# Half of a KAN's activations moved from ScalarE to GpSimd, value tiles cleared once, and a third PSUM bank for the attention's row maxima

## The chip, the core and the metric

The kernel runs on one core of a Trainium2 chip. Its time is device microseconds (us) of that core. The engines are named as in the profile: PE is TensorE's matmul, PEld its weight load, ACT ScalarE, DVE VectorE, POOL GpSimd, SP SyncE (which here only issues DMAs). Each engine works through its own instructions in the order in which the kernel issued them, so an instruction that waits holds up all that stand behind it on its engine.

## What is computed

Sixteen sequences (rows, b = 0 to 15) of 512 tokens with 128 features go through two "macaron" layers. The reference's main lines are:

```
x = x + 0.5 * kan(layernorm(x))                 # s = x@Win + bin; h = relu(s*W1 + b1), 16 values per
                                                # feature; g = sum(h*W2) + b2; out = g@Wout + bout
x = x + attention(layernorm(x))                 # 16 heads of 8, 4 key/value heads, rope, causal softmax
x = x + 0.5 * kan(layernorm(x))
x = x + 0.5 * moe(layernorm(x))                 # 8 experts, each takes its top 128 of 512 tokens
x = x + recurrence(layernorm(x))                # s = l*s + u over the tokens
x = x + 0.5 * moe(layernorm(x))
```

The part that the change touches most is the KAN's inner function, for each of 64 features m with 16 hidden values each:

```
h = relu(s[..., None] * W1 + b1)
g = einsum('btmh,mh->btm', h, W2) + b2
```

Since relu(z + c) = max(z, -c) + c, the sum over h can also be made from max(z, -c), if the sum of c*W2 is added to b2 once.

## The kernel before

**One program of coroutines.** All engine work is issued by Python generators, each of which stands for one stage of one row and gives up its place with `yield`. One round over all of them is a *turn*; `turn()` first issues what was put off to the next turn (`later`, which is where a result leaves PSUM), then steps the urgent stages, then the side stages, then refills a budget per engine. In a turn of the attention phase the main loop (from L1216) steps `weights(b)` and `maxima(b + 1)` once each, and so a row has 4 x 11 = 44 turns. When `paced[0]` is set, a stage that asks with `need(...)` or `bank(...)` for more than the budget has left waits for another turn. The budget of a turn is `MOST = {"pe": 1.5, "dve": 1.15, "act": 0.85, "pool": 1.45}` (L234); the work of `weights` and `maxima` itself isn't in it. After the attention `paced` is off and `hurry` is on.

**Rows in flight.** While `weights(b)` runs, `maxima` works on row b + 1. From turn 38 of row b `stage_in(b + 4)` runs the first KAN and `attn_in` of a later row, and from turn 8 `stage_out(b - 1)` the output projection, the second KAN and the router's scores of the row before. After the 44 turns `finish` makes more turns if `stage_in(b + 2)` isn't through.

**maxima** (L631 to L658): for each of 4 groups of heads, 11 banks of scores are made by bf16 matmuls (L645; L641 first adds the causal mask) and reduced to row maxima by DVE (L650 for a bank of one head, a custom add-and-max with the mask; L655 for shared banks). The banks come from the pool `scp`, which has two; PE can fill a third one only when DVE has read the first. **weights** (L692 to L718) makes the scores a second time, transposed (L709), in two banks of the pool `stp`; ACT takes the exponentials (L712) and POOL sets the masked part of the diagonal block to zero (L714). **outputs** (L720 to L760) multiplies them with the values (L735) a group later.

**kan(b)** (L347 to L409): after a layernorm (L303 to L324; its power of -1/2 runs on POOL, L309 and L310, and the scaling on DVE, L320 or L324), a transpose (L336) and a copy (L338), two matmuls (L356) make both halves of s, each copied to SBUF by ACT (L359). Eight steps follow, spread over 15 turns; each makes one activation of 128x512 on ACT (L389). After the fourth and the eighth step four matmuls (L383) sum four of these values into the bank `ps_kg`, of the pool `kap`, which has one bank and nothing else in it until the experts use it. In the second step POOL adds the constant `kcst` to x (L393). ACT copies the bank to `gT` (L396), four matmuls (L404) project it, DVE adds to x (L405). `kan_held` lets only one KAN at a time have its second half of s.

**attn_in(b)** (L440 to L517): a norm, two matmuls for the query and its rotated form (L448, L454), both multiplied with the rope by DVE (L449, L455) and added by POOL (L470); keys and values (L462, L466). `parts` splits the query and the key into three bf16 terms: a copy on ACT (L414) and three subtractions on POOL (L417, L420, L423). The values go to a fresh tile `va` of four buffers, which POOL first sets to zero (L476), with a column of ones (L479); DVE copies the values in (L484) in the next turn.

**prepare** (L542 on) makes the constants, among them `kcst`, from b2, Wout and bout. **dispatch** (L940 on) transposes gathered tokens for the experts into a PSUM bank `ps_x`: in `ps_kg`'s bank once all KANs are through, in a bank of the shared pool `mm` before that. The pool `mm` has two banks, counted by `held`; nearly all other stages use it.

Of the kernel before, what the change touches and what calls it, by code (L numbers as in the profile page):

```python
# [17 lines left out]
P = 128  # L18
# [30 lines left out]
def tile_macaron(  # L49
# [55 lines left out]
    with ExitStack() as ph:  # L105
# [4 lines left out]
        vap = ph.enter_context(tc.tile_pool(name="p1_va", bufs=4))  # L110
        hp = ph.enter_context(tc.tile_pool(name="p1_h", bufs=5))
# [55 lines left out]
        rbias = cst.tile([P, 2, NV], F32, name="rbias")  # L167

# [36 lines left out]
        ROWS = slice(0, P)  # L205

# [50 lines left out]
        held, kan_held, kans, hurry = [0], [0], [2 * B], [False]  # L257
# [89 lines left out]
        def kan(b):  # L347
# [18 lines left out]
            pg = kap.tile([P, S], F32, name="ps_kg")  # L366
# [3 lines left out]
            for t in range(U + 1):  # L370
                while now[0] < begin + 15 * t // 8:
                    yield
                four = t in (U // 2, U)
                work = {"act": 0.8} if t < U else {}
                if four:
                    work["pe"] = 1.0
                if t == 1:
                    work["pool"] = 1.25
                yield from need(**work)
                if four:  # L380
                    for half, v, h in hs:
                        o = half * M + v % 2 * MH
                        nc.tensor.matmul(pg[o : o + MH, :], lhsT=w2d[:, half, v, :], rhs=h,  # L383
                                         start=(t < U), stop=(t == U))
                    hs = []
                if t < U:
                    half, v = t // 2 % 2, t // 4 * 2 + t % 2
                    h = hp.tile([P, S], F32, name="kan_h")
                    nc.scalar.activation(h, sk[half], AF.Relu, bias=rbias[:, half, v : v + 1],  # L389
                                         scale=kw1[:, half, v : v + 1])  # L390
                    hs.append((half, v, h))
                if t == 1:
                    nc.gpsimd.tensor_tensor(x[b], x[b], kcst.unsqueeze(1).to_broadcast([P, NT, D]), ALU.add)  # L393
                if t == U:
                    gT = hp.tile([P, S], F32, name="kan_h")
                    later.append(lambda: nc.scalar.copy(gT, pg))  # L396
                yield
            take(act=0.6)
            kan_held[0] = 0
            kans[0] -= 1  # L400
# [39 lines left out]
        def attn_in(b, st):  # L440
# [3 lines left out]
            tb = w1p.tile([P, S], F32, name="rope_b")  # L444
# [27 lines left out]
            qp_steps = parts(ta, qpart, nc.scalar.copy, 1.15, act=0.6)  # L472
            step(qp_steps)

            va = vap.tile([P, NT, NR, 32], F32, name="va")
            nc.gpsimd.memset(va, 0.0)  # L476
            mine = [va[:, :, j::2, 2 * HD * j : 2 * HD * (j + 1)] for j in range(2)]
            for to in mine:
                nc.gpsimd.memset(to[:, :, :, HD : HD + 1], 1.0)  # L479
# [10 lines left out]
            st["va"] = va  # L490

            def keys():
# [3 lines left out]
                yield  # L496
                yield
# [44 lines left out]
        def prepare():  # L542

            for half in range(2):
                nc.vector.scalar_tensor_tensor(rbias[:, half, :], in0=kw1[:, half, :], scalar=binc[:, half : half + 1],
                                               in1=kb1[:, half, :], op0=ALU.mult, op1=ALU.add)
            nc.vector.tensor_add(w2d[:, 0, 0:2, :].rearrange("p v m -> p (v m)"), ident[:, 0:M], ident[:, M:P])
# [8 lines left out]
            yield  # L556
            psc = yield from bank([1, D], F32, "ps_kc")
            nc.tensor.matmul(psc, lhsT=kb2, rhs=wout, start=True, stop=True)
# [71 lines left out]

        def maxima(b, st):  # L631
            qp, kp = packed(b)
            for half in range(2):
                maxs = topped[half][:, 0 : NT * NH // 2].rearrange("p (h c) -> p h c", c=NT)
                for r in (2 * half, 2 * half + 1):
                    for c, gs in BANKS:
                        n = (c + 1) * P
                        v = in_bank(scp.tile([P, S], F32, name="ps_sc"), gs)
# [165 lines left out]
        def routing(k, g):  # L804
# [50 lines left out]
            tokf = rtp.tile([P, CAP], F32, name="tokf")  # L855
# [7 lines left out]
            both = rtp.tile([P, 2, P], F32, name="both")  # L863
# [76 lines left out]
        def dispatch():  # L940
            while taken[0] < NR * B:
                yield
            for i in range(0, len(order), 2):
# [5 lines left out]
                own = kans[0] == 0  # L949
                if own:  # L950
# [8 lines left out]
                if not own:  # L959
                    freed()  # L960
# [353 lines left out]
```

## Time and profile before

| | |
|---|---|
| median of 13 runs | 1647.13 us (1639.85 to 1656.4) |
| the profiled execution | 1649.8 us, of which 1646.3 us span |
| busy, share of the span | PE 92%, PEld 64%, DVE 67%, ACT 58%, POOL 57% |
| first exponential (L712), last one | 115.2 us, 937.1 us |
| one row of attention, 349.59 to 403.40 us | 53.81 us: PE 50.11, DVE 42.38, ACT 40.35, POOL 30.30 |
| L389, the KAN's activation, ACT, 128x512 | x256, 816 ns |
| L393, add of kcst, POOL, two inputs, 128x512 | x32, 1277 ns |
| L476, memset of va, POOL, 128x512 | x16, 525 ns |
| L714, mask on POOL, 128x512 and 128x128 | x64, 644 ns and x512, 319 ns |
| L650, maxima on DVE, 128x512 and 128x384 | x256, 682 ns and x256, 549 ns |
| chain that ended last, by engine | PE 70%, DVE 16%, ACT 6%, issue 3%, POOL 3% |

The span is the time from the first to the last instruction of the profiled execution. A group's line in the profile names the line of the kernel, the engine, the operation, output and input, and a count. Busy shares of POOL are rough, and a matmul's end is modelled, so a PE that seems busy may still have gaps. The chain is followed back from the last instruction, at each step to what released it.

### The profile page before, as it was taken

Reading aid. Unit: us, or ns where it says so; the run is one execution under the profiler, and the core shown is the slowest. Engines: PE = TensorE matmul, PEld = TensorE weight load, DVE = VectorE, ACT = ScalarE, POOL = GpSimd, SP = SyncE. Lnnn points to the kernel's source line nnn. Section 1 sums busy time; section 2 is a strip of 40 time slices with the busy share of each in tenths; the row PEclk is TensorE's granted clock in tenths of the full one; section 3 lists DMA queues with packets and bytes.
Section 4 is the critical chain, followed back from the end, with each engine's and each line's share of the span. In section 5 each row is a group of like instructions: output and inputs, shape, how many; then the busy total and the mean of one; then the engine's idle time right before and its main releaser. Section 6 shows DMA issues by size and latency. Waiting matters only on the chain.

```text
span 1646.3 us, 33179 instructions
## 1 busy us (share of the span) xinstructions
PE 1506.7 (92%) x11903; PEld 1052.7 (64%) x11905; DVE 1095.0 (67%) x3574; ACT 957.7 (58%) x1852; POOL 933.1 (57%) x1475
## 2 busy tenths in 40 slices
PE   5678999999999999999989899999999999999998
PEld 2334444445444444444444499899998999889898
DVE  5587878777877788888887255765578555743333
ACT  3345667777777777777767754444453445443343
POOL 2435546555654565456534856556765666666662
PEclk8889999999999999999999999999999999999999
DMA  5311111012101210122022113223222233232332
GB/s 130 88 45 38 45 51 50 20 48 58 49 23 45 58 56 18 44 58 57 26 74 74 30 45 68 64 55 73 63 67 63 61 71 71 62 64 65 65 68 49
DMA packets 107467, 92.87 MB, mean 56 GB/s; under 512 B 23470, under 2 KB 95863, under 8 KB 107063
## 3 DMA queue, kind: packets, MB, share of 16 engines
q1 hardware_dynamic: 84464, 67.67, 14.4%
q0 software_dynamic: 21584, 22.89, 7.6%
q8 instruction: 93, 1.52, 0.4%
q14 instruction: 72, 0.58, 0.1%
q10 hardware_dynamic: 1254, 0.20, 0.1%
HBM read 59.20 MB, written 35.45 MB: 57 GB/s over the span
## 4 chain that ended last, share of the span: by engine, by line
PE 70%; DVE 16%; ACT 6%; issue 3%; POOL 3%; DMA 1%; SPq 1%; another core or an unknown queue 0%; ACTq 0%; DVEq 0%; POOLq 0%
PE ps_y L1041 13%; PE ps_h L1028 13%; PE ps_av L735 7%; DVE below L650 6%; PE ps_st L709 6%; PE ps_sc L645 5%; PE acc L992 5%; PE ps_s L356 3%; PE ps_kg L383 3%; ACT pt L712 3%; PE ps_t L336 3%; DVE ln_st L303 2%; PE ps_x L955 2%; PE ps_g L796 2%; ACT kan_h L389 2%
## 5 line engine op out<-in xcount | busy, mean ns | idle before, releaser
L714 POOL TENSOR_SCALAR_AFFINE_SELECT pt<-pt 128x128 f32<-128x128 f32 (+2 forms) x704 | 256.0, 370 | 346.3 <-ACT pt L712 342.1
L712 ACT ACTIVATE pt<-ps_st 128x512 f32<-128x512 f32 x682 | 366.9, 563 | 116.7 <-PE ps_st L709 115.2
L650 DVE CUSTOM_DVE_ANT_0 below<-ps_sc,causal 128x512 bf16<-128x512 f32 (+1 forms) x512 | 315.3, 616 | 94.8 <-PE ps_sc L645 79.6
L931 POOL DMA_INDIRECT xg<-xnd,tokI x256 | 253.7, 991 | 84.5 <-issue 43.7
L1030 ACT ACTIVATE mo<-ps_h 128x512 f32<-128x512 f32 x256 | 152.8, 597 | 223.0 <-PE ps_h L1028 150.7
L1028 PE MATMUL ps_h<-xin,mw 128*128 128x128 f32 x2048 | 275.9, 277 | 4.9 <-ACT mo L1030 3.0
L1041 PE MATMUL ps_y<-mw,mo 128*128 128x128 f32 x2048 | 273.9, 277 | 6.5 <-DVE ye L1047 5.0
L645 PE MATMUL ps_sc<-kp,qp 96*128 96x512 bf16 (+3 forms) x1024 | 256.2, 302 | 22.2 <-DVE topped L650 17.3
L709 PE MATMUL ps_st<-qp,kp 128*128 128x512 bf16 (+1 forms) x990 | 247.6, 301 | 26.8 <-ACT pt L712 25.1
L1028 PEld LDWEIGHTS ps_h<-xin,mw 128*128 128x128 f32 x2048 | 252.1, 193 | 20.1 <-issue 14.5
L1041 PEld LDWEIGHTS ps_y<-mw,mo 128*128 128x128 f32 x2048 | 251.3, 193 | 10.0 <-DVE ye L1047 6.2
L709 PEld LDWEIGHTS <-kp 128*128 128x128 bf16 x1024 | 94.5, 99 | 186.5 <-issue 167.3
L389 ACT ACTIVATE kan_h<-kan_s,rbias,kw 128x512 f32<-128x512 f32 x256 | 206.9, 816 | 2.2 <-PE ps_kg L383 2.2
L1058 POOL DMA_INDIRECT sum<-mo,tokI x93 | 151.7, 1631 | 90.3 <-issue 26.5
L735 PE MATMUL ps_av<-pt,va 128*32 128x512 f32 (+3 forms) x2048 | 165.7, 441 | 0.8 <-POOL pt L714 0.7
L645 PEld LDWEIGHTS <-qp 96*128 96x128 bf16 x1024 | 95.1, 98 | 102.9 <-issue 79.1
L655 DVE TENSOR_REDUCE topped<-ps_sc 128x2 f32<-128x512 f32 (+1 forms) x192 | 129.7, 687 | 22.0 <-PE ps_sc L645 21.5
L735 PEld LDWEIGHTS ps_av<-pt,va 128*32 128x32 f32 x2048 | 53.4, 109 | 90.5 <-issue 43.3
L310 POOL TENSOR_TENSOR ln_rstd<-ln_rstd,mhalf 128x4 f32<-128x4 f32 x96 | 102.0, 1062 | 8.0
L309 POOL TENSOR_SCALAR ln_rstd<-ln_mv 128x4 f32<-128x4 f32 x96 | 22.1, 230 | 136.8 <-DVE ln_mv L307 134.9
L1047 DVE SCALAR_TENSOR_TENSOR parts<-ps_y,gainT,parts 128x128 fp32r<-128x128 f32 x80 | 27.9, 348 | 98.9 <-ACT parts L1044 76.7
L1047 DVE SCALAR_TENSOR_TENSOR ye<-ps_y,gainT,ye 128x128 fp32r<-128x128 f32 x83 | 29.0, 349 | 89.2 <-ACT ye L1044 61.2
(205 smaller groups left out, 2321.9 us busy)
## 6 DMA issues: line engine op xcount, KB each, us to landing
qp<-qs SPq DMA_DIRECT2D x64, 288.0 KB
xnd<-kan_x SPq DMA_DIRECT2D x32, 256.0 KB
sum<-x SPq DMA_DIRECT2D x62, 128.0 KB
qs<-qpart SPq DMA_DIRECT2D x48, 128.0 KB
kp<-ks SPq DMA_DIRECT2D x48, 96.0 KB
x<-in_L_attn_x_dram SPq DMA_DIRECT2D x16, 256.0 KB
mw<-in_L_ffn_w_dram SPq DMA_DIRECT2D x16, 256.0 KB
xg<-xnd,tokI POOLq DMA_INDIRECT x256
```

The costliest lines, as they stand in the source:

```text
L389: nc.scalar.activation(h, sk[half], AF.Relu, bias=rbias[:, half, v : v + 1], scale=kw1[:, half, v : v + 1])
L645: nc.tensor.matmul(v[:, u, 0:n], lhsT=qp[r][0:MXR, g, bass.ts(c, P)], rhs=kp[0:MXR, r, 0:n], start=alone, stop=(u == len(gs) - 1), skip_gr ...
L650: nc.vector.tensor_tensor_reduce(below[:, 0:n], v[:, 0, 0:n], causal[:, S - n : S], 1.0, LOWEST, ALU.add, ALU.max, accum_out=maxs[:, h, c ...
L709: nc.tensor.matmul(v[:, u, 0:n], lhsT=kp[ROWS, r, bass.ts(c, P)], rhs=qp[r][ROWS, g, c * P : S], start=True, stop=True)
L712: nc.scalar.activation(o, v[:, :, 0:n], AF.Exp, scale=HD ** -0.5)
L714: nc.gpsimd.affine_select(out=dg, in_=dg, compare_op=ALU.is_ge, fill=0.0, base=0, pattern=[[0, len(gs)], [1, P]], channel_multiplier=-1)
L735: nc.tensor.matmul(po[32 * g : 32 * g + 32, c * P : S], lhsT=va[:, c, r, :], rhs=pt[:, g, OFF[c] : OFF[c] + n], start=(c == 0 and not odd) ...
L931: nc.gpsimd.indirect_dma_start(out=xgs[i // E % 2][:, i % E, :], out_offset=None, in_=xnd[b], in_offset=bass.IndirectOffsetOnAxis(ap=tokI[ ...
L1028: nc.tensor.matmul(pst[:, f, :], lhsT=mw1[e][:, bass.ts(f, P)], rhs=xins[i // E % 2][:, i % E, :], start=True, stop=True)
L1030: nc.scalar.activation(hs[u], pst, AF.Gelu)
L1041: nc.tensor.matmul(py, lhsT=hs[u][:, f, :], rhs=mw2[e][:, f, :], start=(f == 0), stop=(f == NF - 1))
L1058: nc.gpsimd.indirect_dma_start(out=sums[k, b], out_offset=bass.IndirectOffsetOnAxis(ap=tokI[g][:, n : n + 1], axis=0), in_=added[b % 2 * ( ...
```

## The change

- **KAN.** Of the eight activations of a KAN the four with odd v are made by POOL as max(W1*s, -c) (by DVE in the last KAN, under `hurry`); the other four stay on ACT. The eight matmuls that sum them all come after the eighth step, four in one turn and four in the next, into a bank of the shared pool `mm` in place of `kap`'s. `hp` holds eight tiles instead of five; `gT` gets a buffer of `kan_s0`. The add of kcst moves from the second to the fifth step.
- **Constants.** `nbias` is -rbias. `prepare` sums c*W2 of the shifted values by four matmuls of one column, doubles that sum (w2d carries a factor of 0.5) and adds b2, and uses the result in b2's place.
- **maxima.** Every third bank comes from `kap`, so three are in rotation. `dispatch` then always uses `kap`'s bank.
- **attn_in.** Four tiles `VA` are fixed; each is set to zero, with its ones, only for rows 0 to 3. The first step of the query's `parts` isn't taken in the turn of POOL's add, but, when paced, two turns later. The key's add then comes one turn later than before and its `parts` two.
- **Buffers.** `rope_b` shares a buffer with `yT`, `tokf` with `probs`, `both` with `wk`.

```diff
-        vap = ph.enter_context(tc.tile_pool(name="p1_va", bufs=4))
-        hp = ph.enter_context(tc.tile_pool(name="p1_h", bufs=5))
+        vap = ph.enter_context(tc.tile_pool(name="p1_va", bufs=1))
+        hp = ph.enter_context(tc.tile_pool(name="p1_h", bufs=8))
...
+        VA = [vap.tile([P, NT, NR, 32], F32, name=f"va{i}", tag=f"va{i}") for i in range(4)]
...
-            pg = kap.tile([P, S], F32, name="ps_kg")
             hs = []
             begin = now[0]
             U = 2 * NV
-            for t in range(U + 1):
+            for t in range(U):
                 while now[0] < begin + 15 * t // 8:
                     yield
...
+                half, v = t // 2 % 2, t // 4 * 2 + t % 2
+                shifted = v % 2
+                yield from need(**({"pool": 0.8} if shifted else {"act": 0.8}))
+                h = hp.tile([P, S], F32, name="kan_h")
+                if shifted:
+                    (nc.vector if hurry[0] else nc.gpsimd).tensor_scalar(
+                        h, sk[half], kw1[:, half, v : v + 1], nbias[:, half, v : v + 1], ALU.mult, ALU.max)
+                else:
                     nc.scalar.activation(h, sk[half], AF.Relu, bias=rbias[:, half, v : v + 1],
                                          scale=kw1[:, half, v : v + 1])
...
-                if t == 1:
+                hs.append((half, v, h))
+                if t == 4:
+                    yield from need(pool=1.25)
                     nc.gpsimd.tensor_tensor(x[b], x[b], kcst.unsqueeze(1).to_broadcast([P, NT, D]), ALU.add)
...
+            pg = yield from bank([P, S], F32, "ps_kg", 1.0)
+            for begins in (True, False):
+                for half, v, h in hs[0:4] if begins else hs[4:8]:
+                    o = half * M + v % 2 * MH
+                    nc.tensor.matmul(pg[o : o + MH, :], lhsT=w2d[:, half, v, :], rhs=h,
+                                     start=begins, stop=not begins)
+                if begins:
+                    yield
+                    yield from need(pe=1.0)
+            gT = w2p.tile([P, S], F32, name="kan_g", tag="kan_s0")
+            later.append(lambda: nc.scalar.copy(gT, pg))
+            kan_held[0] = 0
...
-            qp_steps = parts(ta, qpart, nc.scalar.copy, 1.15, act=0.6)
-            step(qp_steps)
-
-            va = vap.tile([P, NT, NR, 32], F32, name="va")
-            nc.gpsimd.memset(va, 0.0)
+
+            va = VA[b % len(VA)]
             mine = [va[:, :, j::2, 2 * HD * j : 2 * HD * (j + 1)] for j in range(2)]
-            for to in mine:
-                nc.gpsimd.memset(to[:, :, :, HD : HD + 1], 1.0)
+            if b < len(VA):
+                nc.gpsimd.memset(va, 0.0)
+                for to in mine:
+                    nc.gpsimd.memset(to[:, :, :, HD : HD + 1], 1.0)
...
             st["va"] = va
+            if paced[0]:
+                yield
+            qp_steps = parts(ta, qpart, nc.scalar.copy, 1.15, act=0.6)
...
+            psc = yield from bank([P, 1], F32, "ps_kcg")
+            for half in range(2):
+                for v in range(1, NV, 2):
+                    o = half * M + MH
+                    nc.tensor.matmul(psc[o : o + MH, :], lhsT=w2d[:, half, v, :], rhs=rbias[:, half, v : v + 1],
+                                     start=(v == 1), stop=(v == NV - 1))
+            nc.vector.tensor_copy(gcst, kb2)
+            for half in range(2):
+                rows = slice(half * M + MH, (half + 1) * M)
+                nc.vector.scalar_tensor_tensor(gcst[rows, :], in0=psc[rows, :], scalar=2.0, in1=kb2[rows, :],
+                                               op0=ALU.mult, op1=ALU.add)
+            freed()
             psc = yield from bank([1, D], F32, "ps_kc")
-            nc.tensor.matmul(psc, lhsT=kb2, rhs=wout, start=True, stop=True)
+            nc.tensor.matmul(psc, lhsT=gcst, rhs=wout, start=True, stop=True)
...
-                        v = in_bank(scp.tile([P, S], F32, name="ps_sc"), gs)
+                        v = in_bank((kap if turns[0] % 3 == 2 else scp).tile([P, S], F32, name="ps_sc"), gs)
+                        turns[0] += 1
...
-                own = kans[0] == 0
-                if own:
-                    ps = kap.tile([D, 2, CAP], F32, name="ps_x", tag="ps_kg")
-                else:
-                    ps = yield from bank([D, 2, CAP], F32, "ps_x")
+                ps = kap.tile([D, 2, CAP], F32, name="ps_x", tag="ps_sc")
```

## The prediction, made before the changed kernel had run

> **What bounds the kernel now.** I read the page's busy shares and slices first, then the windows of one row of attention, then who waited for whom in four equal rows, the timeline of one row, and the chain of waits beside it.
>
> ```profile
> PE 1506.7 (92%) x11903; PEld 1052.7 (64%) x11905; DVE 1095.0 (67%) x3574; ACT 957.7 (58%) x1852; POOL 933.1 (57%) x1475
> ...
> PE   5678999999999999999989899999999999999998
> ...
> DVE  5587878777877788888887255765578555743333
> ACT  3345667777777777777767754444453445443343
> POOL 2435546555654565456534856556765666666662
> ```
>
> ```profile
> 349.59:403.40 53.81, 50.11 (x402) 25.78 (x406) 42.38 (x137) 40.35 (x76) 30.30 (x65) 1.00 0.16 45
> ...
> 674.64:728.88 54.24, 50.31 (x403) 25.83 (x406) 45.17 (x158) 40.52 (x76) 30.68 (x66) 1.00 0.15 44
> ```
>
> The columns of the second fence are the stretch, its length, then busy PE, PEld, DVE, ACT, POOL, and PE's clock. There are three parts: a fill up to 115 us (the first exponential of L712), attention to about 945 us, experts to the end. The last third has nothing of the change in it except one KAN and moved banks; it is bound by PE (L1028, L1041). In attention a row takes 53.81 or 53.82 us six times over, and PE looks 93% busy. That share flatters PE, since ends of matmuls are modelled. Where the chain runs from PE to PE it shows the real pace: 0.22 us for a 128x512 bf16 matmul, 0.86 for a ps_s, 0.99 for the four ps_kg (shown as x8), 1.43 for the x24 of ps_av, 0.44 for four transposes. Multiplied with the matmuls of the row 363.96 to 417.77 this makes 46.05 us of PE work; **7.76 us of each row are lost.** I cut that row where its chain leaves PE and counted the PE work in each piece:
>
> - A, 363.96 to 372.96: 8.15 us of work, 0.85 lost (a copy and an exponential on ACT).
> - B, 372.96 to 384.12: 8.91 of work, 2.25 lost (ACT, POOL, then DVE to the end).
> - E, 389.90 to 396.40: 4.77 of work, 1.73 lost (DVE throughout).
> - G, 410.73 to 413.77: 1.92 of work, 1.12 lost (ACT: exponentials and two activations of the KAN, 0.70 and 0.48).
> - The remaining 24.1 us, PE behind PE: 0.96 lost, 4%. Nobody takes that away.
>
> ```profile
> PE ps_st L709 <- ACT pt L712: 6.4, 16, 0.6
> ...
> PE ps_sc L641 <- DVE topped L650: 3.6, 8, 0.7
> PE ps_sc L645 <- DVE topped L650: 3.5, 8, 0.6
> ...
> DVE va L484 <- POOL va L476: 7.4, 4, 1.8
> ...
> ACT qpart L414 <- POOL rope_a L470: 6.6, 4, 1.6
> ```
>
> These are sums over four rows. PE's waits are of two kinds: a bank of the maxima that DVE hasn't emptied (L650), a bank of the exponentials that ACT hasn't (L712). Behind the first stands the fourth line: once a row DVE waits 1.84 us for a memset on POOL. The timeline shows it:
>
> ```profile
> 373.20 0.69 DVE L650 CUSTOM_DVE_ANT_0 below<-ps_sc,causal 128x512 bf16<-128x512 f32 x1
> ...
> 373.97 1.27 POOL L470 TENSOR_TENSOR rope_a<-rope_a,rope_b 128x512 f32<-128x512 f32 x1
> ...
> 375.18 0.53 POOL L476 MEMSET va<- 128x512 f32 x1
> ...
> 375.74 0.36 DVE L484 COPY va<-ps_kv 128x64 f32<-128x64 f32 x2 [1.84 <-POOL va L476]
> ...
> 376.02 0.68 DVE L650 CUSTOM_DVE_ANT_0 below<-ps_sc,causal 128x512 bf16<-128x512 f32 x1
> ...
> 390.54 1.56 DVE L320 TENSOR_SCALAR kan_x<-x,ln_mv,ln_rstd 128x128 f32<-128x128 f32 x2
> 390.72 1.30 POOL L393 TENSOR_TENSOR x<-x,kcst 128x512 f32<-128x512 f32 x1
> ```
>
> The memset stands behind the rope's add on POOL, DVE's copies into va behind the memset, and the next maximum behind the copies.
>
> **The change, part by part, for one row.**
>
> 1. *va made once.* Twelve of 16 memsets (525 ns, and two of 115) leave POOL: 0.75 us a row. More important, DVE's copies no longer wait for POOL: 1.84 us of idle DVE at the head of piece B go. DVE sets that piece to its end, so they count up to what PE can use: 8.91 of work with its 4% is 9.3, so 1.86 of the 11.16 can go. I take 1.8. What is late next there is PE itself.
>
> 2. *The query's bf16 copy two turns later.* ACT stood 1.64 us before L414 for POOL's add; a turn is 53.8 / 44 = 1.22 us, so all of that goes. It is hidden under piece B, so nothing more is counted. The three subtractions and DMAs behind it come a turn or two later; stage_in starts four rows ahead and then waits for freed query banks, so this costs nothing. If that cover were gone, it would be 1.2 us a turn.
>
> 3. *Four of eight activations of each KAN on POOL.* Each leaves 0.82 us of ACT (L389); two KANs a row make 6.5 us off ACT's 40.4. This counts only where ACT ends the chain: of the 0.70 and 0.48 in piece G one goes, 0.6 us; in A I take 0.2. Added to POOL are eight tensor_scalar of 128x512. No row shows one. The nearest from below is the 525 ns memset of this size, from above the two-input add of L393 with 1280; one input and one output of this size has L714 with 644 (319 for 128 columns, so 0.85 ns a column over some 0.21). By the latter I take 0.66, and keep 0.53 and 1.28. POOL's row becomes 30.3 - 0.75 + 5.3 = 35 us of some 51 (40 at 1.28), so its sum doesn't bind. Queued behind them are the masks of L714, which ps_av needs about three turns later.
>
> The Trainium skill, "GPSIMD Engine Reference", section 4.1, advises VectorE for elementwise work and calls GpSimd with one input roughly line rate, and section 3.1 gives 769 ns for its best loop over 512 elements; no run here shows that loop. By it POOL would get 6.2 us a row instead of 5.3, an estimate that leaves the sum where it is.
>
> 4. *What the new POOL work does to DVE.* In the last two lines above two L320 take 1.56 us beside POOL's add, against a median of 0.343 each. Over four rows L320 has a mean of 595 ns and L324 one of 799 (median 692): 4 x 0.25 + 3 x 0.11 = 1.3 us a row of DVE time are lost today. L650, with one input in PSUM, doesn't stretch (517 to 693 for its two shapes). Seven such DVE operations a row, a POOL activation under way for 10% of the time, half of 0.66 us to wait: 0.23 us; I take 0.4, since it lands in pieces that DVE sets. Bounds: 0, and 8 x 0.5 = 4.1 (below, rival 2).
>
> The Trainium skill, "SBUF — State Buffer", section "Who interferes with whom", says that GpSimd and VectorE share one port pair that is locked for a whole instruction against VectorE's fast and two-input SBUF operations. The two lines agree with it. If every one of the eight activations held DVE for its whole 0.66 us, it would be 5.3 us a row, an estimate from that rule which would make the change a loss.
>
> 5. *A third bank for the maxima.* PE may be one bank further ahead of DVE before it stops. Piece E is DVE's to its end, and after it 14.3 us follow in which PE leads and DVE can catch up. Its recoverable part is 1.73 - 4% of 6.5 = 1.5 us; one bank is worth up to one turn, 1.2. DVE's products for PE (kan_x, three turns ahead of the transposes) get later by the same backlog, so I take half of 1.5: 0.8. Bounds 0 and 1.5.
>
> 6. *KAN's sums at its end, in a bank of mm.* The same eight matmuls; four move from the middle to the end, two turns before the copy. By the code, mm's two banks are held for some 30 of 88 bank turns a row, so the bank is there. The last POOL activation is issued two turns before its matmul. A KAN holds its second input for 17 turns after against 18 before by the code, two of them in 44 turns. I take 0.
>
> 7. *Constants, at the start.* Four matmuls of one column and four small operations ahead of kcst; the add that needs kcst (POOL waited 10.6 us for it once) moves behind activations. I take 0, bounds -2 and +3 us for the whole fill.
>
> The sum: 1.8 + 0.6 + 0.2 + 0.8 - 0.4 = **3.0 us a row.** Rows 0 to 8: 27 us. In rows 9 to 11 the routing's maxima raise DVE to 45 to 47 us a row, so there is less slack: 2.0 each, 6 us. Rows 12 to 14 have no stage_in, so no piece B: 1.0 each, 3 us. In row 15 the chain holds seven activations of 0.70 us between 925 and 937; half go to POOL, which is 75% busy there: 1.5 us. Together 37.5 us. The profiled execution took 1649.8 us (span 1646.3), so 1612.3; it lay 2.7 above the median 1647.13, so **1610 us.**
>
> **Rivals.**
>
> 1. *Only the one stall goes.* Speaks for it: DVE is 79% busy and its work isn't less; a third bank may only let its backlog grow, and the transposes wait in place of the maxima. With 0.8 lost to that, 1.8 + 0.6 - 0.8 = 1.6 a row: 12 x 1.6 + 3 = 22, so 1625 us.
>
> 2. *The port, slower.* Place: DVE's kan_x operations (L320, L324) in the pieces that DVE sets. Today two adds of 1.28 us a row go with 1.3 us lost, at most 0.65 for one; I price one meeting at 0.5. If an activation is as long as that add and each one meets such an operation, 8 x 0.5 = 4.1 us are lost against 3.4 gained, and DVE's delay is passed to PE: 0.7 x 12 = 8 us, 1655 us. It decides from 0.43 us lost for each activation. Against it: seven such operations of 0.3 to 0.7 us don't fill a row.
>
> 3. *It doesn't get there: the planner.* L714 isn't in POOL's plan, and an activation needs 0.8 of 1.45, so beside a norm (1.4) or a subtraction (1.15) it waits a turn. If KANs grew past 22 turns each, the row's end would wait for stage_in and eat the gain: 1647 us. Against it: by the code about ten turns of 44 are taken in this way, and a KAN's POOL activations are almost four turns apart.
>
> **How the numbers follow.** A measurement of this kernel can tell about 0.3%, 5 us, from no change. Forecast (1590 to 1622): 55%. Rival 1 (1622 to 1640): 17%. More than forecast, all of 1.86 + 1.5 + 1.1 + 0.5 a row, below 1590: 5%. No change, rival 3: 8%. Slower, rival 2: 15%. So faster 77%, same 8%, slower 15%. The range must reach from the upper bound of the gain (4.96, so 5.0 x 12 + 5 = 65, 1582) to no gain, 1648, which leaves out the slower case.
>
> **What would show it.** Right: no wait of DVE for va after row 3; PE's waits for DVE topped under half; a row of about 51 us; L389 half as many on ACT; POOL's new tensor_scalar at 0.6 to 0.8 us. L320 and L324 above 600 and 800 ns would show rival 2; transposes (ps_t) waiting for kan_x, rival 1; gaps over 3 us between ps_st matmuls at a row's end (the largest now is 2.27), rival 3. I am wrong if the pieces that DVE sets stay as long as they are though its wait for va is gone.

## The result and the profile after

The changed kernel takes **1690.78 us** (median of 10 runs, 1681.67 to 1699.51), before 1647.43 (46 runs): a ratio of **1.0265, 95% interval 1.0247 to 1.0282**. It is 43 us slower, where 37 us less were forecast; the profiled execution has a span of 1688.7 us.

The page of the changed kernel, the busy shares, POOL's slices, the chain by engine, and the group of the new instruction (count | busy us, mean ns | idle time before it):

```profile
PE 1534.3 (91%) x11910; PEld 1061.9 (63%) x11913; DVE 1085.5 (64%) x3582; ACT 876.9 (52%) x1724; POOL 1171.3 (69%) x1563
...
POOL 5745658787878788787875775657666676656672
...
PE 65%; POOL 16%; DVE 14%; issue 2%; ACT 2%; another core or an unknown queue 0%; DMA 0%; ACTq 0%; DVEq 0%; POOLq 0%
...
L381 POOL TENSOR_SCALAR kan_h<-kan_s,kw,nbias 128x512 f32<-128x512 f32 x124 | 263.2, 2123 | 15.7 <-ACT kan_s L363 15.6
```

ACT lost 81 us of work, as meant. POOL gained 238: 263 for the new instruction, less some 25 of memsets and masks (L739, 240.5 us for 256.0). It takes **2.12 us each time, where the prediction had 0.66 and an upper bound of 1.28.** POOL's share of the chain that ended last went from 3% to 16%.

A row, in the columns of the prediction's windows:

```profile
332.63:387.61 54.98, 50.72 (x403) 26.06 (x406) 41.61 (x137) 35.55 (x68) 45.32 (x70) 1.00 0.16 44
```

54.98 us instead of 53.81; POOL is busy for 45.32 of them (30.30 before). The sum of a row therefore doesn't say that POOL is the bound: 9.7 us are free. PE's waits for POOL and DVE over four rows (us in total, times, longest), and in the second fence its weight load's wait in front of the KAN's sums, show where it is:

```profile
PE ps_kg L395 <- POOL kan_h L381: 3.7, 4, 0.9
PE ps_m L690 <- DVE topped L680: 2.7, 4, 0.7
PE ps_t L340 <- DVE kan_x L328: 2.2, 4, 0.5
PE ps_sc L666 <- DVE topped L675: 2.1, 4, 0.5
```

```profile
PEld ps_kg L395 <- POOL kan_h L381: 7.3, 4, 1.8
```

PE's waits for the maxima of L675 fell from 7.1 us to 2.1; with the new wait of ps_m for L680 it is 4.8. Also new is that once a row PE stops in front of the KAN's sums until POOL's last activation is there. The lines of PE and of its weight load are the same stop, seen twice: both end at 381.87 us in the row shown, where the weight load has had nothing for 1.8 us and PE for 0.9. So 0.9 to 1.8 us a row are waited there. The chain of waits in this row (start, length, engine, line) shows why that activation is late:

```profile
366.81 2.08 POOL kan_h L381
...
372.28 2.08 POOL kan_h L381
...
374.85 1.24 POOL x L389
...
376.59 2.06 POOL kan_h L381
378.65 1.11 POOL pt L739 x4
379.76 2.07 POOL kan_h L381
381.83 0.04 issue
381.87 1.05 PE ps_kg L395 x2
```

Between 365.5 and 381.8 us POOL is idle for less than 0.1 us in all: two norms (L314), four activations, the masks (L739) and the add of kcst stand one behind the other, and PE waits for the end of that queue. Shares of the row average that away.

To set the kernels of this study side by side I cut their time at three marks: the first exponential (the **fill** ends), the last one (the **rows**), and the first activation of an expert (the **end** of the last KAN). The expert part goes by the chip used: from its start to the end the profiled executions of e9 to e12 took 660 to 663 us, those of e5 to e7 on another chip 698 to 701. So times are compared up to its start, and ratios only with the kernel before on the same chip. Each row of times is one profiled execution, so differences of about 1 us are weak evidence; e2 and e14, on two chips, agree within 0.2 us in fill, rows and end.

| us | fill | rows | end | start of experts | ratio (95%) |
|---|---|---|---|---|---|
| before | 115.2 | 821.9 | 8.4 | 945.5 | 1 |
| after | 132.4 | 839.0 | 19.9 | 991.3 | 1.0265 (1.0247 to 1.0282) |
| e2, activations on ScalarE | 116.8 | 806.6 | 8.7 | 932.1 | 0.9898 (0.9878 to 0.9919) |
| e3, on VectorE | 121.9 | 831.8 | 8.1 | 961.8 | 1.0097 (1.0080 to 1.0114) |
| e4, GpSimd's share alone | 130.8 | 944.6 | 16.0 | 1091.4 | 1.0915 (1.0895 to 1.0935) |
| e5, after with the short form | 120.6 | 810.8 | 15.9 | 947.3 | 1.0008 (0.9986 to 1.0030) |
| e6, va alone | 114.8 | 819.2 | 8.4 | 942.4 | 0.9968 (0.9945 to 0.9991) |
| e7, banks and sums alone | 116.4 | 810.9 | 8.5 | 935.8 | 0.9945 (0.9920 to 0.9970) |
| e9, e2 in the change's order | 116.5 | 807.7 | 8.1 | 932.3 | 0.9909 (0.9886 to 0.9932) |
| e10, e5 in e2's order | 122.1 | 798.5 | 15.8 | 936.4 | 0.9946 (0.9929 to 0.9962) |
| e11, GpSimd in the rows alone | 114.1 | 840.8 | 8.6 | 963.5 | 1.0124 (1.0107 to 1.0141) |
| e12, two of eight on VectorE | 118.5 | 802.3 | 7.2 | 928.0 | 0.9898 (0.9881 to 0.9914) |
| e13, e9 with unread GpSimd work | 116.6 | 808.5 | 8.5 | 933.6 | 0.9921 (0.9895 to 0.9947) |
| e14, e2 with unread GpSimd work | 116.6 | 806.6 | 8.7 | 931.9 | 0.9898 (0.9868 to 0.9928) |

After against before, the 45.8 us up to the experts are 17.2 in the fill, 17.1 in the rows and 11.5 at the end: more is lost in the few KANs at the two ends than in the long middle, where nearly all of the forecast was made. Against the forecast it is the rows that miss most: 17.1 lost where 36 gained had been summed. Nor do all rows lose the same: from their first exponential to the next row's, the six equal rows take 1.16 us more each, the third row of all 5.5 (64.21 against 58.69).

### The profile page after: what moved, and what is told of

The parts are those of the page before. It is cut to its first block, busy times and chain, and to the rows that moved or that the text cites. A ratio compares the mean times of both kernels' runs of the same rounds, so it can differ in the third digit from the quotient of the medians.

```text
span 1688.7 us, 33263 instructions
## 1 busy us (share of the span) xinstructions
PE 1534.3 (91%) x11910; PEld 1061.9 (63%) x11913; DVE 1085.5 (64%) x3582; ACT 876.9 (52%) x1724; POOL 1171.3 (69%) x1563
## 4 chain that ended last, share of the span: by engine, by line
PE 65%; POOL 16%; DVE 14%; issue 2%; ACT 2%; another core or an unknown queue 0%; DMA 0%; ACTq 0%; DVEq 0%; POOLq 0%
PE ps_y L1060 12%; PE ps_h L1047 12%; PE ps_av L760 7%; POOL kan_h L381 7%; PE ps_st L734 5%; PE acc L1011 5%; PE ps_sc L670 4%; POOL pt L739 3%; PE ps_kg L395 3%; DVE below L675 3%; PE ps_s L360 3%; PE ps_t L340 2%; DVE ln_st L307 2%; POOL ln_rstd L314 2%; DVE topped L680 2%
## 5 line engine op out<-in xcount | busy, mean ns | idle before, releaser
L675 DVE CUSTOM_DVE_ANT_0 below<-ps_sc,causal 128x512 bf16<-128x512 f32 (+1 forms) x512 | 314.8, 615 | 134.1 <-PE ps_sc L670 120.3
L739 POOL TENSOR_SCALAR_AFFINE_SELECT pt<-pt 128x128 f32<-128x128 f32 (+2 forms) x704 | 240.5, 357 | 169.6 <-ACT pt L737 166.0
L381 POOL TENSOR_SCALAR kan_h<-kan_s,kw,nbias 128x512 f32<-128x512 f32 x124 | 263.2, 2123 | 15.7 <-ACT kan_s L363 15.6
L680 DVE TENSOR_REDUCE topped<-ps_sc 128x2 f32<-128x512 f32 (+1 forms) x192 | 127.4, 684 | 26.6 <-PE ps_sc L670 24.9
L395 PE MATMUL ps_kg<-kan_h,w2d 128*32 128x512 f32 x512 | 100.7, 656 | 33.6 <-POOL kan_h L381 31.8
L314 POOL TENSOR_TENSOR ln_rstd<-ln_rstd,mhalf 128x4 f32<-128x4 f32 x96 | 102.0, 1062 | 8.0
L384 ACT ACTIVATE kan_h<-kan_s,rbias,kw 128x512 f32<-128x512 f32 x128 | 102.8, 808 | 0.0
## 6 DMA issues: line engine op xcount, KB each, us to landing
xnd<-kan_x SPq DMA_DIRECT2D x32, 256.0 KB
x<-in_L_attn_x_dram SPq DMA_DIRECT2D x16, 256.0 KB
mw<-in_L_ffn_w_dram SPq DMA_DIRECT2D x16, 256.0 KB
```

What stands on the lines that cost most here:

```text
L381: (nc.vector if hurry[0] else nc.gpsimd).tensor_scalar(h, sk[half], kw1[:, half, v : v + 1], nbias[:, half, v : v + 1], ALU.mult, ALU.max)
L675: nc.vector.tensor_tensor_reduce(below[:, 0:n], v[:, 0, 0:n], causal[:, S - n : S], 1.0, LOWEST, ALU.add, ALU.max, accum_out=maxs[:, h, c ...
L680: nc.vector.tensor_reduce(maxs[:, h : h + len(gs), c], v[:, :, 0:n], AX.X, ALU.max)
L739: nc.gpsimd.affine_select(out=dg, in_=dg, compare_op=ALU.is_ge, fill=0.0, base=0, pattern=[[0, len(gs)], [1, P]], channel_multiplier=-1)
```

## The experiments

The theory is **length**: GpSimd needs 2.1 us for this one form of instruction. Its rivals are the **port** (the activation is long because VectorE and GpSimd block one another), **order** (the planner places things differently when activations are booked as GpSimd's), and the **next wait** (the other parts brought a new stall).

**e1, the instruction by itself.** No part of the reference is computed: x is copied through, and each form runs four times on an engine while all others are idle.

```diff
+    for e in (nc.gpsimd, nc.vector):
...
+        ts(e, S, a, m, ALU.mult, ALU.max)
...
+        ts(e, S, a, m, ALU.mult, ALU.add)
+        ts(e, S, 0.5, 0.25, ALU.mult, ALU.max)
...
```

> A small kernel that computes nothing of the reference: it copies x through, and on an otherwise idle core GpSimd makes tensor_scalar of 128x512 float32, first as the change has it (times a per-partition value, then max with another), then narrower, with constants in place of per-partition values, with one operation, and with add for max; then VectorE makes the same. Theory 'length' (the operation itself takes 2.1 us on GpSimd, whatever the other engines do): about 2.08 us at 512 columns, near 0.23 + 3.6 ns a column, so 1.15 at 256 and 0.7 at 128. Theory 'port' (it is short, and is stretched by VectorE's work beside it): 0.6 to 0.8 us at 512 here. Which of the variants is cheap is open; 0.65 is expected for those with one operation under either theory. VectorE: 0.54 us for the change's form, as in the last KAN of the changed kernel.

POOL's timeline in e1 (start, length). The lines are the forms mult-then-max and mult-then-add with their numbers in a column of SBUF, and the same two with constants:

```profile
35.87 2.07 POOL L74 TENSOR_SCALAR h<-s,w 128x512 f32<-128x512 f32 x1
...
51.94 0.77 POOL L74 TENSOR_SCALAR h<-s,w 128x512 f32<-128x512 f32 x1
...
54.92 1.92 POOL L74 TENSOR_SCALAR h<-s 128x512 f32<-128x512 f32 x1
...
62.46 0.62 POOL L74 TENSOR_SCALAR h<-s 128x512 f32<-128x512 f32 x1
```

Alone on an idle core the activation takes 2.07 us: it is the form, not the company. Mult-then-add of the same bytes takes 0.77. VectorE needs 0.54 for mult-then-max.

**e2, without GpSimd's share.** All other parts of the change stay; all eight activations are ScalarE's.

```diff
-                shifted = v % 2
+                shifted = 0
...
-            nc.tensor.matmul(psc, lhsT=gcst, rhs=wout, start=True, stop=True)
+            nc.tensor.matmul(psc, lhsT=kb2, rhs=wout, start=True, stop=True)
```

> The changed kernel with all eight activations of a KAN on ScalarE, unshifted, and b2 in place of the summed constant; everything else of the change stays (three banks, sums at the end, value tiles cleared once, the later copies). Theory 'length': GpSimd's activations are the whole loss, and the other parts gain what I worked out without the 0.6 + 0.2 of ACT and without the 0.4 of the port, so 1.8 + 0.8 = 2.6 us a row: 1610 to 1622 us, a row of 51 to 52 us. Theory 'rest' (the sums at the end or the third bank cost as well): 1640 us or more.

0.9898: the rest of the change is a gain of 1%, and moving the activations costs 59.2 us of 991.3. The expected 1610 to 1622 us were worked out from a kernel before of 1647, so they mean 0.978 to 0.985: the rest gains, but less than had been worked out. Two rows of e2, which alternate, and all that PE waits ScalarE for in four rows:

```profile
372.93:476.98 104.05, 99.15 (x800) 51.38 (x804) 81.99 (x272) 80.77 (x151) 58.43 (x124) 1.00 0.15 46
```

```profile
PE ps_st L734 <- ACT pt L737: 8.3, 18, 0.9
```

The two rows together make 52.02 us each, and PE no longer waits for a maximum at all. What is left is ScalarE's exponentials, 2.1 us a row: the theory of the next wait falls as the cause of the loss. That relieving ScalarE would be right in itself is argued from this line; e10 and e12 try it.

**e3, the four activations on VectorE.** One could say that the shift is good and only the engine is wrong.

```diff
-                    (nc.vector if hurry[0] else nc.gpsimd).tensor_scalar(
+                    nc.vector.tensor_scalar(
```

> The changed kernel with the four shifted activations of every KAN on VectorE (0.54 us each, so 4.3 us a row) instead of GpSimd; the planner still books them as GpSimd's. Theory 'length': GpSimd's queue is free again, VectorE rises from 41.6 to 46 us a row, so a row of 51 to 53 us and 1615 to 1645 us. Theory 'rest': no better than 1680 us.

1.0097, rows of 54.09 and 55.63, above the expected range (0.981 to 0.999 of before): VectorE, which sets the pieces B and E, gets 4.3 us more a row (8 x 0.54), and PE's waits for it over four rows go from 0.8 us in e2 to 11.5.

**e4, GpSimd's share without the other parts.** The kernel before, with the shifted activations and their constants, and the add of kcst moved as in the change.

> The kernel before with only the activations' part of the change: four of eight on GpSimd, shifted, with their summed constants, the add of kcst in the fifth step; sums in two halves in their own bank, two banks for the maxima, value tiles cleared each time. Theory 'length': as slow as the whole change or slower, since the other parts' gain is missing and the middle sum waits for GpSimd too: 1695 to 1725 us. Theory 'rest': within 1% of before.

1.0915, a row of some 64.5 us, well above the expected range (1.029 to 1.047 of before). Here four values are summed after the fourth and four after the eighth step, and the weight load waits for POOL's activation at every one of these sums: 16 times in four rows, 30.3 us in total. The other parts together, worth 13.4 us without GpSimd (e2), are worth 100.1 with it (991.3 against 1091.4). That most of this is part 6, the sums at the KAN's end, which the prediction costed at nothing, is argued from that: no run takes part 6 alone.

**e5, the changed kernel with the short form.** It isn't the same function: half of the activations are scaled and shifted but not clipped. All engines' instructions keep their order; only the length differs.

```diff
-                        ... nbias[:, half, v : v + 1], ALU.mult, ALU.max)
+                        ... nbias[:, half, v : v + 1], ALU.mult, ALU.add)
```

> The changed kernel with add in place of max in the shifted activations, on GpSimd: half of the KAN's values are then not clipped, so part of the computation is left out; nothing else differs. Alone on the core this form took 0.77 us, against 2.07 with max. Theory 'length' (the change lost by the length of this one form): a row of 50 to 51 us, below the kernel with all activations on ScalarE: 0.970 to 0.985 of before. Theory 'queue' (four more instructions a KAN on GpSimd cost through its in-order queue or the shared port, whatever their length): at or above 1.00.

The instruction in e5 (minimum, median and maximum in ns), and one row:

```profile
L381 POOL TENSOR_SCALAR kan_h<-kan_s,kw,nbias x124: 758/768/1288, 18.0 to 936.5; 128x512 f32<-128x512 f32 x124
```

```profile
300.21:353.21 53.00, 49.65 (x403) 25.98 (x406) 41.46 (x137) 35.53 (x68) 35.53 (x71) 1.00 0.16 45
```

991.3 us to the experts became 947.3. Of the 45.8 us lost **44.0 are the length of this one form**: 11.8 in the fill, 28.2 in the rows, 4.0 at the end. PE's other three waits in the fence of PE's waits above (2.7, 2.2 and 2.1 us) are the same in e5; only the wait for POOL is gone. But even so there is no gain: 1.0008 and rows of 53.00, where theory 'length' had 0.970 to 0.985 and 50 to 51. Of the 83 us between the forecast (37.5 gained) and the 45.8 lost up to the experts, the length is 44. The other 39 are there with the short form too: 25 in the rows (11.1 gained, 36 summed), 9 at the end, 5.4 in the fill.

**e6, va made once, alone.** The kernel before with the four tiles `VA`, cleared in rows 0 to 3; the query's copy stays where it was.

> The kernel before with one part alone: the four value tiles are cleared in rows 0 to 3 only; the copies of query and key stay where they were. By part 1 of the prediction, 1.8 us in each of 12 rows, 22 us: 0.987 of before. Theory 'next wait' (another wait, ScalarE's for GpSimd's rope add or a bank of the maxima, takes the place of the one removed): 0.995 to 1.00.

0.9968, a row of 53.44: 0.37 us, where 1.8 were counted; all rows together gain 2.7. DVE no longer waits for the memset, and something else takes its place:

```profile
ACT qpart L416 <- POOL rope_a L472: 6.5, 4, 1.6
```

The chain of this kernel goes in piece B through POOL's add, this copy (0.62 us), one exponential and PE's ps_st. ScalarE stands 1.6 us a row behind the add, and the exponentials behind ScalarE: over four rows PE waits 7.9 us for them, before 6.4. The prediction had counted this wait as covered.

**e7, third bank and sums at the end, alone.** e2 with the memset in every row and the query's `parts` as before.

> All activations on ScalarE, three banks for the maxima and the KAN's sums at its end, but value tiles cleared in each row and the copies of query and key where they were before. By part 5 of the prediction, 0.8 us a row: 0.990 to 0.994 of before. Theory 'ScalarE next' (VectorE's banks are waited for no more, and ScalarE, with all eight activations, sets the row instead): 0.996 to 1.004, and the gain of the kernel with all activations on ScalarE comes from the value tiles.

0.9945, between the ranges of the two theories; the rows take 11.0 us less, 0.73 each on average. Of these 4.8 are the third row alone (53.85 against 58.69); the six rows that were equal before now alternate between 50.15 and 55.81 or 57.39, and gain 0.57 each. From e7 to e2, where va and the later copy come together, the rows lose 4.3 us more, 0.29 each.

**e8, more forms.** As e1, with nothing of the reference computed.

> Computes nothing of the reference. More forms on GpSimd alone, 128x512: tensor_tensor multiply by a broadcast value; tensor_scalar with max then mult, add then max, mult then subtract; mult then max and mult then add with bfloat16 out; a copy. Theory 'max' (max is slow): about 2 us for the two forms with max and about 0.8 for mult then subtract. Theory 'one fast form' (only mult then add has fast code): about 2 us for mult then subtract too. The copy 0.5 to 0.8, bfloat16 as float32.

```profile
L74 POOL TENSOR_SCALAR h<-s,w 128x512 f32<-128x512 f32 x12 | 24.7, 2073 | 0.0
...
L93 POOL COPY h<-s 128x512 f32<-128x512 f32 x4 | 2.3, 612 | 0.0
```

The first line is max-then-mult, add-then-max and mult-then-subtract, four of each: all are as long as mult-then-max. With an output in bf16 nothing changes (2.07 for the long form, 0.77 for mult-then-add).

**e9 and e10, order by itself.** In e9 every activation is ScalarE's but half are booked as GpSimd's, so the order is that of the change. In e10 GpSimd has the short form (half of the values unclipped, as in e5), booked as ScalarE's, so the order is that of e2. In the traces up to the experts PE's and DVE's instructions do stand in these orders.

The lines of e9 (which also has b2 in place of the summed constant, as e2), and then of e10 (with `ALU.add`):

```diff
-                shifted = v % 2
-                yield from need(**({"pool": 0.8} if shifted else {"act": 0.8}))
+                shifted = 0
+                yield from need(**({"pool": 0.8} if v % 2 else {"act": 0.8}))
```

```diff
-                yield from need(**({"pool": 0.8} if shifted else {"act": 0.8}))
+                yield from need(act=0.8)
```

> The kernel with all activations on ScalarE (e2) but with the odd ones booked in the planner as the change books them, 0.8 of GpSimd's budget instead of ScalarE's. TensorE's instructions then stand in the changed kernel's order, GpSimd has no activation. Theory 'order' (the changed booking puts the stages of a row into an order in which VectorE's norms fall together, and that costs the row 1 us against e2): a row of 52.8 to 53.5 us, 0.997 to 1.004 of before. Theory 'GpSimd' (the activations on GpSimd cost through its queue or port even at 0.77 us): a row of 52.0 us as in e2, 0.988 to 0.993.

> The kernel of e5 (add in place of max on GpSimd, 0.77 us, half of the values not clipped) but booked in the planner as ScalarE's work, so that TensorE's instructions stand in the order of e2. Theory 'order': the gain shows that I had forecast for a short activation, a row of 50.5 to 51.5 us, 0.980 to 0.988 of before. Theory 'GpSimd': a row of 53 us, 0.997 to 1.003.

Order alone costs 1.1 us in the rows (807.7 against 806.6); e9's ratio of 0.9909 is in the range of theory 'GpSimd', its row of 52.77 at the edge of 'order'. With GpSimd at work it costs 12.3 (e5 810.8, e10 798.5). So e10 shows what the prediction had in mind, if less of it than theory 'order' expected (0.9946, not 0.980 to 0.988): with the short form and this order the rows gain 8.1 us on e2. The fill and the end give that back (5.3 and 7.1), and the start of the experts is 4.3 later than in e2.

**e11, GpSimd in the rows alone.** In the fill's KANs and the last row's, ScalarE makes all eight (in these KANs the constants are counted twice).

```diff
-                if shifted:
+                if shifted and not (filling[0] or taken[0] > NR * (B - 1)):
```

> The changed kernel, with max on GpSimd, except that the KANs of the fill and the one in row 15 make all their activations on ScalarE, unshifted (the summed constant then counts twice in those KANs, so their values are off). The order of TensorE's instructions is that of the change. Theory 'three places' (of the changed kernel's 46 us until the experts begin, 17 come in the fill and 12 in row 15, where GpSimd has each other work queued behind, and 17 in the rows between): first exponential at 115 to 120 us instead of 132, 1.007 to 1.013 of before. Theory 'rows' (what isn't lost at the start is lost later, since the rows wait for GpSimd anyway): 1.020 or more.

963.5 instead of 991.3: fill and end are back to the old 114.1 and 8.6, the rows stay at 840.8. So the three stretches add up separately, as theory 'three places' had it (1.0124).

**e12, two of eight on VectorE.** e3 with only v = 3 shifted, booked with 0.5 us of VectorE's plan.

> The changed kernel with only two of a KAN's eight activations shifted (v = 3), on VectorE at 0.54 us, booked as 0.5 of VectorE; GpSimd has none. ScalarE set some of e2's row, and it loses 3.3 us a row here, while VectorE gets 2.2. Theory 'ScalarE next': a row of 51 to 51.7 us and 0.982 to 0.988 of before, the best so far. Theory 'order': the stages fall differently again, and the row may be anything from 51 to 53.5; 0.985 to 1.000.

0.9898, as e2: in the range of theory 'order', not in that of 'ScalarE next' (0.982 to 0.988); 928.0 to the experts against 932.1. Both beat the kernel before and the changed one; which of the two is better these runs, on two chips, can't say.

**e13 and e14, GpSimd's work with nobody waiting.** e9 and e2, and for each shifted activation GpSimd makes a mult-then-add of 416 columns into a tile that is never read (0.72 us each).

```diff
+                if v % 2 and not hurry[0]:
+                    nc.gpsimd.tensor_scalar(
+                        dump, sk[half][:, 0:416], kw1[:, half, v : v + 1], nbias[:, half, v : v + 1], ALU.mult, ALU.add)
```

> The kernel of e9 (every activation on ScalarE, half of them booked as GpSimd's, so in the changed kernel's order), and GpSimd makes four mult-then-add of 128x416 for each KAN into a tile that nobody reads, at the places where the change has its activations (about 0.65 us each). Nothing waits for them. Theory 'port' (it is GpSimd's instructions at these places that hold up VectorE, whatever they are for): VectorE's two-input norm operation, mean 0.68 us in e9 and 0.88 in e5, goes to 0.85 or more; TensorE's waits for the maxima and for kan_x come back, about 7 us in four rows as in e5; first to last exponential 815 us or more against 807.7 in e9. Theory 'place' (it is what follows from ScalarE doing half as much, another order in time, and not GpSimd's work): 0.70 us or less, no such waits, 807 to 810 us.

> The same four unread instructions on GpSimd in the kernel of e2, whose order has all activations booked as ScalarE's. Theory 'port' with the place deciding: the two-input norm operation at 0.72 us as in e10, first to last exponential 806 to 809 us against 806.6 in e2. If GpSimd's additional work costs in any order: 812 us or more in both e13 and e14.

VectorE's two-input norm operation over four rows, in e9 and then in e13:

```profile
L328 DVE TENSOR_TENSOR kan_x<-x,ln_rstd 128x512 f32<-128x512 f32 x12 | 8.1, 679 | 0.0
```

```profile
L329 DVE TENSOR_TENSOR kan_x<-x,ln_rstd 128x512 f32<-128x512 f32 x12 | 10.2, 849 | 0.0
```

GpSimd's instructions do stretch it, by 0.17 us (while the mean of the one-input norm operation falls from 419 to 339 ns), and PE's wait for kan_x grows from 0.7 to 1.9 us in four rows. That half of "port" holds. Its price doesn't: the rows take 808.5 us against 807.7. In e2's order the operation stays at 0.72 us and the rows at 806.6. So the port by itself doesn't make the 12.3 us between e5 and e10. PE's waits for ps_m and ps_sc, 4.8 us in four rows of e5, are in neither e9 nor e13; they show only where ScalarE is relieved and this order is kept. Why is not settled.

## Why the prediction was wrong

**Part 3, the length of GpSimd's activation, is the step that failed.** It said "one input and one output of this size has L714 with 644" and bounded the price by 0.53 and 1.28. All three rows were other operations, and it measured 2.12. The trace of before had no tensor_scalar of this form on POOL, and its cost depends on the pair of operations: 0.77 or 2.07 us for the same bytes (e1, e8). "So its sum doesn't bind" was true even at 2.07 (45.3 of 54.98), and misled: what binds is the stretch of 16 us in which POOL's queue is unbroken. By e5 this term is 44.0 us. It isn't the whole miss: with 0.77 us, inside the prediction's bounds, the kernel still gains nothing (e5), for the steps in the table below.

The Trainium skill, "GPSIMD Engine Reference", section 4.1, calls one-input work on GpSimd roughly line rate, and section 3.1 has a loop over 512 elements at 769 ns. In the runs mult-then-add takes 767 ns, close to that figure, though no run shows that it is that loop; mult-then-max (2067 ns), and the other pairs of e8 (2073 ns on average), don't come near it.

The other steps, in us of a row unless said otherwise:

| step | predicted | measured |
|---|---|---|
| 1, 2: va once, later copy | -1.8 | -0.37 (va alone, in the equal rows), -0.29 (both, beside the bank) |
| 5: third bank | -0.8 | -0.73 (with the sums) |
| 3, 4: activations moved | -0.8 + 0.4 | +2.16 (rows of after against e2, by 15); +0.28 with the short form |
| 7: fill | 0 (-2 to +3) | +1.6 in e2; +17.2 with GpSimd |
| last row's KAN | -1.5 in all | +11.5 in all |

- **Parts 1 and 2.** The wait for va did vanish (once after, in the first rows). Wrong was to give the whole piece B to it, and nothing to the copy. They are two waits of about the same end, POOL's add, and take turns: e6 removes one and the other stays. With both gone beside the third bank, 0.29 remains. That the bank had already let PE run over the same gap is a reading that no run tests, and none has the later copy alone. The pieces on record also don't add up: A, B, E, G and the rest make 6.91 us and not 7.76, so if the four are right, the remaining 24.1 us lose 1.81 and not 0.96. With that share piece B could give 1.6 and not 1.86, which is still far above what e6 measured.
- **Part 4 and rival 2.** The place was right and the price wrong (8 x 0.5 is 4.0, too, and not 4.1). In the changed kernel L324 (L320 before) has a mean of 390 ns against 595, and L328 (L324 before) 876 against 799:

```profile
L328 DVE TENSOR_TENSOR kan_x<-x,ln_rstd 128x512 f32<-128x512 f32 x12 | 10.5, 876 | 1.8 <-POOL ln_rstd L314 1.8
```

By the same sum over the medians, 4 x 0.05 + 3 x 0.18 = 0.7 us a row are lost, less than the 1.3 before. The activation takes 2.12 in the rows and 2.07 alone. Of its two signs one came (L328 above 800 ns) and one didn't (L324 above 600). The loss had the rival's direction and not its mechanism.
- **Part 5** was right in size on average, in part by luck: in e7 the equal rows gain 0.57, and 4.8 of the 11.0 us come from the third row alone. **Part 6** was right as long as ScalarE delivers (e7). With GpSimd, PE's one wait for it stands here, since two turns between activation and matmul don't cover an unbroken queue of 16 us; by e4 it would probably be worse without.
- **Part 7.** The constants do fit the bounds (e2: +1.6). Forgotten was that the KANs of the fill have the same four activations, when nothing else hides them. The chain of the changed kernel's fill:

```profile
108.55 2.06 POOL kan_h L381
110.61 0.41 POOL rope_ka L425
...
111.51 2.06 POOL kan_h L381
113.57 0.04 issue
113.62 1.06 PE ps_kg L395 x2
```

POOL holds the fill's norms, rope, `parts` and activations in one line; the first exponential comes 17.2 us later, and 5.4 later with the short form (e5). PE's granted clock fell with it: 0.78 over the fill against 0.85 before and 0.84 in e5, and the fill's matmuls take 87.4 us of PE against 76.4 and 76.8. How much of the 11.8 us between e5 and the change the clock makes, no run shows.
- **The last row's KAN** was a gain of 1.5 by the count of ScalarE's activations in the chain. The row said "POOL, which is 75% busy there" and the sum didn't use it. The activations stand behind the experts' fetches (xg) and the masks:

```profile
977.45 1.02 POOL xg L956
...
979.26 2.07 POOL kan_h L381
981.32 0.04 issue
981.37 1.92 PE ps_kg L395 x2
```

Even with the short form the end is 7.5 us longer than before (e5). Here too the clock is lower: 0.74 in this stretch, 0.79 in e5, 1.00 before, and the last line's two matmuls take 1.92 us where the row above has 1.05.
- **Rival 3**, the planner's order, costs 1.1 us by itself (e9), not 37; only together with the activations on GpSimd it is 12.3 (e5 against e10), for a reason that stays open. **Rival 1** doesn't show in e2, whose waits have no transpose behind kan_x; in the changed kernel it is 2.2 us in four rows.

Of the signs that were named, the wait for va and the halved L389 (now L384, x128) came as said. PE's waits for topped came in half: for the maxima of L675 they went to under a third, but with the new wait for L680 it is 4.8 of 7.1. The row (54.98 for 51) and the instruction (2.12 for 0.6 to 0.8) didn't come.

## What to carry to other kernels

Before work is moved to another engine, time that very instruction there, with its operations, types and operands; a row of the same size and another operation is not a bound. Then look at the receiving engine's longest unbroken queue, not at its busy share, and count the move in every stage it occurs in, the fill and the last pass too, where nothing hides it. A stall whose end has a second waiter isn't worth its length: look what stands next behind the same event before counting it.

## What the runs showed of the hardware

- GpSimd, 128x512 f32, on an idle core: copy 0.61 us, mult-then-add 0.77 (0.62 with constants), two-input add or mult 1.04, a single mult or max 1.48 to 1.56, mult-then-max 2.07 (1.92 with constants). One operation is slower than the pair mult, add. The long form takes 0.79 us for 128 columns and 1.21 for 256, so an estimated 3.3 ns a column.
- VectorE, the same: mult-then-max 0.54, with constants 0.42, two-input add 0.69. Three of these adds ran beside GpSimd's last instructions in e1 and took 1.09.
- GpSimd's unread instructions of 0.72 us (e13) stretched a two-input operation of VectorE from 0.68 to 0.85 us on average, while the rows took 0.8 of 808 us more.
